# A graph and convolution layer on one core: residual add in each batch's turn, prefetch across groups, sums and norms in small pieces

## The chip, the cores and the metric

The kernel runs on one core of a Trainium2 chip. TensorE (PE) multiplies matrices, VectorE (DVE), ScalarE (ACT) and GpSimd (POOL) do the elementwise work, and SyncE (SP) issues all DMAs here from one queue. Each engine works through its own list of instructions in the order in which the program wrote them. The metric is device time in microseconds for one execution, the median of several runs.

## What is computed

Input `x` has 32 batches of 512 positions by 256 channels; `adj` is a 0/1 mask of 512 by 512 for each batch. All is in float32.

```python
h = maximum(layernorm(x), 0)                    # h is the layer's input; x the residual
# branch 1: convolution along the positions
c = relu(bn1(conv1d(h, conv1_w)))               # 1 tap
x_conv = relu(bn2(conv1d(c, conv2_w, pad=8)) + h)   # 17 taps, then the residual add
# branch 2: message passing
s = h @ w_se.T + b_se                           # 3 numbers for each position
A = exp(-|s_n - s_m|^2) * adj
x_nmp = A @ relu(h @ w_msg.T + b_msg)
# gated unit over both
gi = concat(x_conv, x_nmp) @ w_ih.T + b_ih;  gh = h @ w_hh.T + b_hh
r, z = sigmoid(...), sigmoid(...);  n = tanh(gi_n + r * gh_n)
out = x + (1 - z) * n + z * h
```

## The kernel before

The 32 batches are worked in 8 groups of 4 (`G`). Three kinds of work are written for each group:

- `rows(g)`: for each batch of group g, load `x` (`load`, L91), normalise it on DVE (`norm`, L174), transpose it on PE (`norm_t`, L189), store the transposed `h` to DRAM (`HD`), and run the 1-tap convolution (`conv1`, L201) into the tile `h1`, which holds one whole group.
- `convolution()` (L368): the 17-tap convolution of a whole group by a nested interpolation scheme with 5 x 5 products. DVE makes the operands `x2` from `h1`, four ahead; weights come from DRAM (`w<-wd`), two ahead; PE multiplies into `ps_c` (three buffers). `summed(g)` (L311) is a generator that takes each of the 25 products from PSUM and sums them into `y`. After the 25th, it evicts `y` to `xconv` for all four batches on ACT (L357, two instructions for each batch), then adds `h` on DVE (L361) and applies ReLU on ACT (L362). For this add, `h` of each batch is loaded from DRAM again (`load_h`, L99) into the tile `hTb`, which has two buffers.
- `rest(b, following)` (L478): all else for one batch. `positions` (L423) makes the tiles `left` and `right`, each partly on DVE (L426, L427) and partly as squares on ACT (L428, L429). Then come `messages` (L431), `kernel_exp` (L442, a matmul of `left` and `right` and an exponential on ACT), `finish` of the batch before (L460), `masked` (L447: transposes of the mask, multiplied in on DVE), the gather and the gates (L520 to L557), of which three elementwise operations for each half are on POOL (L552 to L554). After `masked`, the mask (`load_adj`, one buffer) and `h` of the `following` batch are loaded. The last batch of a group has no `following`.

The order is written out by hand: the main loop (L605 to L653) takes a step of `convolution()` for group g or of `others(g)` (the `rest` of group g-1 and `rows(g+1)`), in proportion to their estimated TensorE time. In `others(g)`, three batches' `rest` come first, then `rows(g+1)`, then the fourth `rest`. So the instructions of a group's last convolution step are followed by the four evictions, and then by `positions` of the group's first batch. Groups 1 to 6 repeat this in the same form. At the end, the four batches of the last group run through `rest` alone.

Of the kernel before, what the change touches and what calls it, by code (L numbers as in the profile page):

```python
# [8 lines left out]
F32 = mybir.dt.float32  # L9
# [31 lines left out]
def kernel(  # L41
# [47 lines left out]
    XS, MS, HB, XR = {}, {}, {}, {}  # L89

    def load(b):  # L91
        XS[b] = front.tile([P, NT, D], F32, name="x_sb")
        nc.sync.dma_start(XS[b], x[b].rearrange("(c p) d -> p c d", p=P))

    def load_adj(b):
# [4 lines left out]
        HB[b] = late.tile([P, ND, N], F32, name="hTb", bufs=2)  # L100
        nc.sync.dma_start(HB[b], HD[b])

    load(0)
    load(1)
    vec = const.tile([P, _NCOL], F32)
    nc.sync.dma_start(vec, vecs)
    w1 = const.tile([P, ND, D], F32)
# [63 lines left out]
    HT = {}  # L171
    HD = {b: dram.tile([P, ND, N], F32, name=f"hd{b}") for b in range(B)}

    def norm(b):  # L174
        xs = XS[b]
        st = front.tile([P, NT, 6], F32, name="st")
        mv = front.tile([P, NT, 2], F32, name="mv")
        for c in range(NT):
            nc.vector.bn_stats(st[:, c, :], xs[:, c, :])
            nc.vector.bn_aggr(mv[:, c, :], st[:, c, :])  # L180
        rstd = front.tile([P, NT], F32, name="rstd")
        rsqrt(rstd, mv[:, :, 1])
        for c in range(NT):
            nc.vector.tensor_scalar(  # L184
                xs[:, c, :], xs[:, c, :], mv[:, c, 0:1], rstd[:, c : c + 1],
                op0=ALU.subtract, op1=ALU.mult,
            )

    def norm_t(b, d):  # L189
        xn = XS[b]  # L190
        if d == 0:
            HT[b] = front.tile([P, ND, N], F32, name="hT")
        ps = tr.tile([P, N], F32, name="ps_tr")
        for c in range(NT):
# [110 lines left out]
    def weights_again():  # L305
        for n in range(25):
            w = cv.tile([P, 2, ND, D], F32, name="w", bufs=3)
            nc.sync.dma_start(w, WD[n])
            yield w

    def summed(g):  # L311

        y = cv.tile([P, 3, 3, NZ], F32, name="y")
        for j1 in ORDER:
            z = y[:, 0] if j1 == 3 else cv.tile([P, 3, NZ], F32, name="z")
            ends = z[:, 0:3:2, :]
# [3 lines left out]
            ps = yield  # L320
            nc.vector.tensor_tensor(z[:, 0, :], ps, n3, op=ALU.add)  # L321
            ps = yield
            nc.vector.scalar_tensor_tensor(z[:, 2, :], n3, 4.0, ps, op0=ALU.mult, op1=ALU.add)
            ps = yield
            n2 = cv.tile([P, NZ], F32, name="n", bufs=3)
            nc.scalar.activation(n2, ps, AF.Copy)
            ps = yield
            s = cv.tile([P, NZ], F32, name="s")
            nc.vector.tensor_tensor(s, ps, n2, op=ALU.add)
            nc.vector.tensor_tensor(n2, ps, n2, op=ALU.subtract)  # L330
            nc.vector.tensor_tensor(ends, ends, s[:, None, :].to_broadcast([P, 2, NZ]), op=ALU.add)  # L331
            nc.vector.scalar_tensor_tensor(z[:, 1, :], n3, 2.0, n2, op0=ALU.mult, op1=ALU.add)
            zf = z.rearrange("p e n -> p (e n)")
            yf = y.rearrange("p f e n -> p f (e n)")
            if j1 == 3:
                nc.scalar.activation(yf[:, 1], zf, AF.Copy, scale=2.0)
                nc.scalar.activation(yf[:, 2], zf, AF.Copy, scale=4.0)
            elif j1 == 0:
                nc.vector.tensor_tensor(yf[:, 0], yf[:, 0], zf, op=ALU.add)
            elif j1 == 4:  # L340
                nc.vector.tensor_tensor(yf[:, 2], yf[:, 2], zf, op=ALU.add)
            else:
                ye = yf[:, 0:3:2, :]
                nc.vector.tensor_tensor(
                    ye, ye, zf[:, None, :].to_broadcast([P, 2, 3 * NZ]), op=ALU.add
                )
                nc.vector.tensor_tensor(  # L347
                    yf[:, 1], yf[:, 1], zf, op=ALU.subtract if j1 == 2 else ALU.add
                )
        if late is None:  # L350
            late_pools()
        for b in range(g * G, (g + 1) * G):
            load_h(b)
            xc = XC[b] = late.tile([P, ND, 9 * U], F32, name="xconv", bufs=4)
            for o in range(ND):
                c = o * NU + b % G * U
                nc.scalar.activation(  # L357
                    xc[:, o, :].rearrange("p (u e f) -> p f e u", e=3, f=3), y[:, :, :, c : c + U],
                    AF.Identity, bias=bn2_sh[:, o : o + 1], scale=bn2_sc[:, o : o + 1],
                )  # L360
            nc.vector.tensor_tensor(xc[:, :, :N], xc[:, :, :N], HB.pop(b), op=ALU.add)  # L361
            nc.scalar.activation(xc[:, :, :N], xc[:, :, :N], AF.Relu)  # L362
        yield

    AHEAD, AHEAD_W = 4, 2
# [2 lines left out]
    def convolution():  # L368

        x2s, ws = [], []  # L370

        def all_operands():
            for _ in range(NG):
                yield from operands()

        def all_weights():
            yield from weights_first()
            for _ in range(NG - 1):
                yield from weights_again()

        xs, wg = all_operands(), all_weights()
        for g in range(NG):
            sums = summed(g)
            next(sums)
            done = None
            for n in range(25):
                while len(ws) < min(25 * g + n + 1 + AHEAD_W, 25 * NG):
                    ws.append(next(wg))

                while len(x2s) < min(25 * g + n + 1 + AHEAD, 25 * NG):  # L390
                    if len(x2s) == 25 * (g + 1):
                        yield "rows", g + 1
                    x2s.append(next(xs))
                    if len(x2s) == 25 * g + 21:
                        yield "free", g
                w, x2 = ws[25 * g + n], x2s[25 * g + n].rearrange("p (r v) -> p r v", v=V)
                ps = cps.tile([P, NZ], F32, name="ps_c")
                for o in range(ND):
                    matmul_sum(
                        ps[:, o * NU : (o + 1) * NU].rearrange("p (b u) -> p b u", u=U),  # L400
                        [
                            (w[:, k, i, o * P : (o + 1) * P], x2[:, i * G : (i + 1) * G, k : k + U])
                            for k in range(2)
                            for i in range(ND)
                        ],
                    )
                    if o == 0 and done is not None:
                        sums.send(done)
                    yield "pe", 1.65
                ws[25 * g + n] = x2s[25 * g + n] = None  # L410
                done = ps
            sums.send(done)
            yield "group", g
# [64 lines left out]
    def rest(b, following):  # L478
# [7 lines left out]
        xnmp = late.tile([P, ND, N], F32, name="xnmp")  # L486
        positions(b)
        yield 1.75
        for c in range(0, NT, 2):
            messages(b, msg, c)  # L490
            yield 1.8
# [12 lines left out]
        if following is not None:  # L504
            load_adj(following)
            load_h(following)
        hT, xconv = HB.pop(b), XC.pop(b)
        o_sb = late.tile([P, ND, N], F32, name="o_sb")
        x_in = [xconv[:, i, :N] for i in range(ND)] + [xnmp[:, i, :] for i in range(ND)]

        def cols(o, g):
            return slice(g * D + o * P, g * D + (o + 1) * P)
# [44 lines left out]
            yield 3.46  # L557
        waiting.append((b, o_sb))

    def rows(g):  # L560

        bs = list(range(g * G, (g + 1) * G))
        for b in bs[:2]:
            if b not in XS:
                load(b)
            norm(b)
        yield 0.0
        for n, b in enumerate(bs + [None]):
            if b is not None:
                for d in range(ND):  # L570
                    norm_t(b, d)
                    yield 0.55
            if n > 0:
                for o in range(ND):
                    conv1(bs[n - 1], o)
                    yield 1.73
            if n + 2 < G:
                load(bs[n + 2])
                norm(bs[n + 2])


    bn1_sc, bn1_sh = bn_affine("bn1")
# [3 lines left out]
        brz, vec[:, _COL["b_ih"] : _COL["b_ih"] + 2 * ND], vec[:, _COL["b_hh"] : _COL["b_hh"] + 2 * ND],  # L586
        op=ALU.add,
    )
    for _ in rows(0):
        pass  # L590

    def others(g):


        bs = list(range((g - 1) * G, g * G)) if g > 0 else []
        for b in bs[:-1]:
            yield from rest(b, b + 1)
# [112 lines left out]
```

## Time and profile before

| | |
|---|---|
| median of 3 runs | 2826.82 us (2824.49 to 2827.24) |
| the profiled execution's own time | 2832.12 us |
| its span, first to last instruction | 2830.3 us |
| PE busy | 2429.8 us, 86% |
| DVE, ACT, POOL busy | 1233.2, 651.2, 310.0 us |
| mean granted TensorE clock | 0.931 |

The profile describes one execution. Its own time is 5.3 us above the median of the runs, and 1.8 us of it lie outside the span. Busy shares are averages over eight groups, the start and the tail.

### The profile page before, as it was taken

To read this page: it belongs to the slowest core of one execution; us is meant where nothing else is said; L and a number is where in the kernel's file an instruction comes from. 1 tells how busy PE (TensorE), PEld (TensorE's weight loads), DVE (VectorE), ACT (ScalarE), POOL (GpSimd) and SP (SyncE) were. 2 spreads that over 40 slices of the span, in tenths; PEclk is the share of its full clock that TensorE was granted. 3 is DMA by queue.
4 is the path that set the end of the run, shared out by engine and by line. 5 is a ranking of instruction groups with operands and counts; after the bars stand their busy time and mean duration, and the time that the engine had idled before them with its cause. 6 is when DMAs were issued, how large, how long until landed. Compare 5 with 4: busy or idle time off the path is not lost.

```text
span 2830.3 us, 20941 instructions
## 1 busy us (share of the span) xinstructions
PE 2429.8 (86%) x8192; PEld 1498.6 (53%) x8192; DVE 1233.2 (44%) x1750; ACT 651.2 (23%) x882; POOL 310.0 (11%) x240
## 2 busy tenths in 40 slices
PE   6568998789986999959989599895998969995998
PEld 4555555456653665536656366563665546653444
DVE  7973345333453344534444434434344444433211
ACT  3232212122122211222212321123222132113221
POOL 1000111101111011011110111100111001111111
PEclk9888998889998999979999899998999989998999
DMA  4242223122232222222232222322223132212210
GB/s 184 104 160 91 88 74 104 60 97 82 89 104 83 80 82 97 90 82 82 82 104 82 90 86 95 101 75 97 82 82 104 60 104 89 82 52 67 75 37 23
DMA packets 113605, 247.95 MB, mean 88 GB/s; under 512 B 8930, under 2 KB 58210, under 8 KB 112866
## 3 DMA queue, kind: packets, MB, share of 16 engines
q1 hardware_dynamic: 113506, 246.60, 25.4%
q8 instruction: 65, 1.06, 0.2%
q14 instruction: 34, 0.28, 0.0%
HBM read 199.91 MB, written 46.66 MB: 87 GB/s over the span
## 4 chain that ended last, share of the span: by engine, by line
PE 77%; DVE 14%; ACT 4%; issue 3%; DMA 2%; POOL 1%; POOLq 0%; SPq 0%; DVEq 0%; ACTq 0%
PE ps_acc L86 49%; PE ps_c L86 18%; PE ps_tr L452 3%; PE ps_acc L444 3%; PE ps_tr L86 2%; DVE x L217 2%; ACT xconv L357 2%; PE ps_tr L195 2%; DVE x L220 1%; DMA hTb<-hd 1%; DVE xconv L361 1%; DVE y L347 1%; DVE z L331 1%; DVE y L468 1%; ACT xconv L362 1%
## 5 line engine op out<-in xcount | busy, mean ns | idle before, releaser
L86 PEld LDWEIGHTS ps_c<-x,w 128*128 128x128 f32 x3200 | 620.7, 195 | 182.1 <-issue 150.1
L86 PE MATMUL ps_c<-x,w 128*128 128x228 f32 x3200 | 694.4, 363 | 24.2 <-DVE z L321 8.2
L86 PE MATMUL ps_acc<-hTb,whh 128*128 128x512 f32 x768 | 361.8, 596 | 0.0
L86 PE MATMUL ps_acc<-xconv,wih 128*128 128x512 f32 x768 | 360.8, 592 | 0.0
L86 PE MATMUL ps_acc<-xnmp,wih 128*128 128x512 f32 x768 | 360.6, 592 | 0.0
L552 POOL TENSOR_TENSOR gate_t<-hTb,r 128x512 f32<-128x512 f32 x64 | 92.4, 1444 | 2276.4 <-ACT r L546 1510.2
L86 PE MATMUL ps_tr<-hTb,wse 128*67 128x512 f32 x128 | 74.3, 711 | 227.6 <-DMA hTb<-hd 200.2
L533 DVE SCALAR_TENSOR_TENSOR r<-ps_acc,vec,r 128x512 f32<-128x512 f32 x64 | 48.1, 751 | 449.9 <-ACT r L531 449.9
L86 PEld LDWEIGHTS ps_acc<-xnmp,wih 128*128 128x128 f32 x768 | 145.3, 189 | 184.3 <-issue 184.3
L86 PEld LDWEIGHTS ps_acc<-xconv,wih 128*128 128x128 f32 x768 | 145.8, 190 | 157.3 <-issue 156.9
L86 PE MATMUL ps_acc<-at,msg 128*128 128x512 f32 x512 | 228.5, 592 | 0.0
L545 DVE TENSOR_TENSOR r<-ps_acc,r 128x512 f32<-128x512 f32 x64 | 44.3, 692 | 399.9 <-PE ps_acc L86 399.7
L86 PEld LDWEIGHTS ps_acc<-hTb,whh 128*128 128x128 f32 x768 | 145.2, 192 | 115.3 <-issue 114.5
L531 ACT ACT_TABLE_LOAD x32 | 41.1, 1283 | 642.0 <-PE ps_acc L86 642.0
L220 DVE SCALAR_TENSOR_TENSOR x<-x,x 128x471 f32<-128x471 f32 (+1 forms) x184 | 158.5, 861 | 5.3
L86 PEld LDWEIGHTS ps_tr<-hTb,wse 128*67 128x67 f32 x128 | 19.5, 160 | 263.1 <-DMA hTb<-hd 205.9
L217 DVE TENSOR_TENSOR x<-x 128x471 f32<-128x471 f32 x200 | 157.7, 807 | 1.4
L86 PEld LDWEIGHTS ps_acc<-at,msg 128*128 128x128 f32 x512 | 97.2, 190 | 106.4 <-issue 106.2
L458 DVE COPY xnmp<-ps_acc 128x512 f32<-128x512 f32 x64 | 44.3, 692 | 246.6 <-PE ps_acc L86 246.6
L444 PE MATMUL ps_acc<-right,left 67*128 67x512 f32 x256 | 124.5, 614 | 14.7 <-ACT at L445 8.7
L195 PE MATMUL ps_tr<-ident,x_sb 128*128 128x128 f32 x256 | 56.3, 365 | 89.8 <-DVE x_sb L184 68.5
L541 ACT ACTIVATE z<-ps_acc,brz 128x512 f32<-128x512 f32 x64 | 44.0, 687 | 337.1 <-PE ps_acc L86 337.1
(94 smaller groups left out, 2312.0 us busy)
## 6 DMA issues: line engine op xcount, KB each, us to landing
w<-wd SPq DMA_DIRECT2D x175, 512.0 KB, 3.3
hTb<-hd SPq DMA_DIRECT2D x64, 512.0 KB, 5.1
m_sb<-in_adj_dram SPq DMA_DIRECT2D x32, 1024.0 KB, 5.6
x_sb<-in_x_dram SPq DMA_DIRECT2D x32, 512.0 KB, 4.4
hd<-hT SPq DMA_DIRECT2D x32, 512.0 KB, 2.9
y<-in_x_dram SPq DMA_DIRECT2D x64, 256.0 KB, 4.0
out_dram<-y SPq DMA_DIRECT2D x64, 256.0 KB, 2.3
wd<-w SPq DMA_DIRECT2D x25, 512.0 KB, 2.8
```

The costliest lines, as they stand in the source:

```text
L86: nc.tensor.matmul(ps, lhsT, rhs, start=(i == 0), stop=(i == len(pairs) - 1))
L195: nc.tensor.transpose(ps[:, c * P : (c + 1) * P], xn[:, c, d * P : (d + 1) * P], ident)
L217: nc.vector.tensor_tensor(dst, get(a), get(b), op=ALU.subtract)
L220: nc.vector.scalar_tensor_tensor(dst, a, -2.0, b, op0=ALU.mult, op1=ALU.add)
L357: nc.scalar.activation(xc[:, o, :].rearrange("p (u e f) -> p f e u", e=3, f=3), y[:, :, :, c : c + U], AF.Identity, bias=bn2_sh[:, o : o + ...
L444: nc.tensor.matmul(ps, left[:, c * P : (c + 1) * P], right, start=True, stop=True)
L452: nc.tensor.transpose(ps[:, n * P : (n + 1) * P], m[:, n, c * P : (c + 1) * P], ident)
L458: nc.vector.tensor_copy(xnmp[:, d, :], ps)
L533: nc.vector.scalar_tensor_tensor(r, ps_h, vec[:, _COL["b_hh"] + 2 * ND + o : _COL["b_hh"] + 2 * ND + o + 1], r, op0=ALU.add, op1=ALU.mult,)
L541: nc.scalar.activation(z, ps_z, AF.Sigmoid, bias=brz[:, ND + o : ND + o + 1])
L545: nc.vector.tensor_tensor(r, ps_n, r, op=ALU.add)
L552: nc.gpsimd.tensor_tensor(t, hT[:, o, :], r, op=ALU.subtract)
```

## The change

It does the following:

- `x_sb` gets three buffers in place of two, and three batches are loaded at the start.
- `norm` becomes a generator that yields between pieces of two to four DVE instructions. `rows_begin(g)` loads the first three batches of a group and enters their norms in `NORMS`; it is called when `rest` of the third batch begins. Each step of `others` first issues one piece (`norm_some`). `norm_all` issues what is left when the batch is transposed. The fourth batch is loaded and entered inside `rows`.
- In `summed`, the additions that do not read PSUM are entered in `SUMS`. One piece is issued at each second half of a convolution step, the remainder before the next products that need the tile `z`, and all of them at the end of the group. Where one addition wrote two thirds of `y` and a second the last third, there are now three.
- The residual add and its ReLU move from `summed` into `rest`, behind `positions`, with the `h` that `rest` has anyway. The separate loads of `h` in `summed` go.
- The last batch of a group now has the next group's first batch as `following`, so its mask and `h` are loaded after `masked` of the last batch.

```diff
     def load(b):
-        XS[b] = front.tile([P, NT, D], F32, name="x_sb")
+        XS[b] = front.tile([P, NT, D], F32, name="x_sb", bufs=3)
...
-    load(0)
-    load(1)
+    for b in range(3):
+        load(b)
...
+    NORMS = {}
+
     def norm(b):
...
             nc.vector.bn_aggr(mv[:, c, :], st[:, c, :])
+            if c % 2:
+                yield
         rstd = front.tile([P, NT], F32, name="rstd")
         rsqrt(rstd, mv[:, :, 1])
+        yield
         for c in range(NT):
...
+            if c % 2:
+                yield
+
+    def norm_some(pieces=1):
+
+        for b in list(NORMS):
+            while pieces and b in NORMS:
+                pieces -= 1
+                if next(NORMS[b], "done") == "done":
+                    del NORMS[b]
+
+    def norm_all(b):
+        if b in NORMS:
+            for _ in NORMS.pop(b):
+                pass
 
     def norm_t(b, d):
         xn = XS[b]
         if d == 0:
+            norm_all(b)
...
+    SUMS = []
+
+    def sum_some(pieces=1):
+        while SUMS and pieces:
+            SUMS.pop(0)()
+            pieces -= 1
+
     def summed(g):
...
             ps = yield
+            sum_some(len(SUMS))
+            z = y[:, 0] if j1 == 3 else cv.tile([P, 3, NZ], F32, name="z")
...
-            nc.vector.tensor_tensor(ends, ends, s[:, None, :].to_broadcast([P, 2, NZ]), op=ALU.add)
-            nc.vector.scalar_tensor_tensor(z[:, 1, :], n3, 2.0, n2, op0=ALU.mult, op1=ALU.add)
+            add(ends, ends, s[:, None, :].to_broadcast([P, 2, NZ]))
+            twice(z[:, 1, :], n3, n2)
...
-                ye = yf[:, 0:3:2, :]
-                nc.vector.tensor_tensor(
-                    ye, ye, zf[:, None, :].to_broadcast([P, 2, 3 * NZ]), op=ALU.add
-                )
-                nc.vector.tensor_tensor(
-                    yf[:, 1], yf[:, 1], zf, op=ALU.subtract if j1 == 2 else ALU.add
-                )
+                for e in range(3):
+                    add(yf[:, e], yf[:, e], zf, ALU.subtract if (e, j1) == (1, 2) else ALU.add)
+        sum_some(len(SUMS))
...
         for b in range(g * G, (g + 1) * G):
-            load_h(b)
...
-            nc.vector.tensor_tensor(xc[:, :, :N], xc[:, :, :N], HB.pop(b), op=ALU.add)
-            nc.scalar.activation(xc[:, :, :N], xc[:, :, :N], AF.Relu)
...
                     if o == 0 and done is not None:
                         sums.send(done)
+                    else:
+                        sum_some()
                     yield "pe", 1.65
...
         positions(b)
         yield 1.75
+        xc = XC.pop(b)
+        xconv = xc[:, :, :N]
+        nc.vector.tensor_tensor(xconv, xconv, HB[b], op=ALU.add)
+        nc.scalar.activation(xconv, xconv, AF.Relu)
         for c in range(0, NT, 2):
             messages(b, msg, c)
...
+    def rows_begin(g):
+
+        for b in range(g * G, g * G + 3):
             if b not in XS:
                 load(b)
-            norm(b)
-        yield 0.0
+            NORMS[b] = norm(b)
+
+    def rows(g):
+
+        bs = list(range(g * G, (g + 1) * G))
...
+                if n == 0:
+                    load(bs[3])
+                    NORMS[bs[3]] = norm(bs[3])
...
-            if n + 2 < G:
-                load(bs[n + 2])
-                norm(bs[n + 2])
...
+    rows_begin(0)
     for _ in rows(0):
-        pass
+        norm_some()
...
-        for b in bs[:-1]:
+        for n, b in enumerate(bs[:-1]):
+            if n == 2 and g + 1 < NG:
+                rows_begin(g + 1)
             yield from rest(b, b + 1)
+        if not bs:
+            rows_begin(g + 1)
         yield "rows wanted", g + 1
...
         for b in bs[-1:]:
-            yield from rest(b, None)
+            yield from rest(b, b + 1)
...
+            norm_some()
             got = next(other, None)
```

## Rows read from the trace of the kernel before

**Rows 1.** The page, part 1: busy us (share of the span) and instructions.
```profile
PE 2429.8 (86%) x8192; PEld 1498.6 (53%) x8192; DVE 1233.2 (44%) x1750; ACT 651.2 (23%) x882; POOL 310.0 (11%) x240
```
**Rows 2.** Waits over the whole span: who waited for whom, us, times, longest.
```profile
PE ps_tr L86 <- DMA hTb<-hd: 200.2, 7, 29.7
...
PE ps_tr L195 <- DVE x_sb L184: 68.5, 9, 14.6
...
PE ps_tr L86 <- issue: 27.4, 1, 27.4
...
PE ps_tr L195 <- issue: 21.3, 9, 2.7
```
**Rows 3.** Timeline over one group's end: start us, us, instruction, [idle before, releaser].
```profile
537.98 29.81 SPq L101 DMA_DIRECT2D hTb<-hd  x4
...
548.91 0.62 DVE L329 TENSOR_TENSOR s<-ps_c,n 128x456 f32<-128x456 f32 x1
...
549.89 1.27 POOL L552 TENSOR_TENSOR gate_t<-hTb,r 128x512 f32<-128x512 f32 x1 [17.27 <-ACT r L546]
...
553.76 3.95 DVE L344 TENSOR_TENSOR y<-y,z 128x2736 f32<-128x2736 f32 x1
557.64 1.57 DVE L347 TENSOR_TENSOR y<-y,z 128x1368 f32<-128x1368 f32 x1
559.24 2.35 ACT L357 ACTIVATE xconv<-y,bn_shift,bn_scale 128x513 f32<-128x513 f32 x2 [9.50 <-DVE y L347]
...
572.06 0.32 SPq L101 DMA_DIRECT2D hTb<-hd  x1
...
577.66 3.68 PE L86 MATMUL ps_tr<-hTb,wse 128*67 128x512 f32 x4 [29.40 <-DMA hTb<-hd]
...
582.87 0.68 ACT L428 ACTIVATE right<-ps_tr,bse 3x512 f32<-3x512 f32 x1 [5.15 <-DVE right L427]
...
588.59 3.60 PE L444 MATMUL ps_acc<-right,left 67*128 67x512 f32 x8
```
**Rows 4.** Timeline at the start of a group's rows.
```profile
784.53 1.70 PE L86 MATMUL ps_c<-x,w 128*128 128x228 f32 x8
...
792.27 2.30 PE L195 MATMUL ps_tr<-ident,x_sb 128*128 128x128 f32 x8 [6.03 <-DVE x_sb L184]
...
799.21 2.81 PE L86 MATMUL ps_c<-x,w 128*128 128x228 f32 x8
...
801.86 3.60 PE L86 MATMUL ps_acc<-hT,w 128*128 128x512 f32 x8
```
**Rows 5.** Timeline where the third batch's `rest` begins.
```profile
707.67 0.94 SPq L474 DMA_DIRECT2D y<-in_x_dram  x2
...
718.77 1.88 PE L86 MATMUL ps_tr<-hTb,wse 128*67 128x512 f32 x4
...
725.48 3.60 PE L444 MATMUL ps_acc<-right,left 67*128 67x512 f32 x8
...
731.84 1.25 PE L452 MATMUL ps_tr<-ident,m_sb 128*128 128x128 f32 x8 [0.35 <-DVE y L468]
```
**Rows 6.** Instructions grouped by line and shape: busy us, mean ns, idle before.
```profile
L179 DVE BATCH_NORM_STATS2 st<-x_sb 128x6 f32<-128x256 f32 x128 | 51.4, 401 | 22.2 <-DMA x_sb<-in_x_dram 22.0
...
L184 DVE TENSOR_SCALAR x_sb<-x_sb,mv,rstd 128x256 f32<-128x256 f32 x128 | 44.2, 410 | 37.2 <-POOL rstd L143 36.0 <-PE ps_acc L86 1.2
...
L361 DVE TENSOR_TENSOR xconv<-xconv,hTb 128x1024 f32<-128x1024 f32 x32 | 39.3, 1227 | 100.1 <-ACT xconv L357 100.1
...
L362 ACT ACTIVATE xconv<-xconv 128x1024 f32<-128x1024 f32 x32 | 33.9, 1058 | 41.4 <-DVE xconv L361 41.4
...
L180 DVE BATCH_NORM_AGGREGATE mv<-st 128x2 f32<-128x6 f32 x128 | 23.3, 182 | 4.4
```
**Rows 7.** Timeline at the start and inside the first group.
```profile
25.45 0.43 DVE L179 BATCH_NORM_STATS2 st<-x_sb 128x6 f32<-128x256 f32 x1 [5.12 <-DMA x_sb<-in_x_dram]
...
140.45 2.30 PE L195 MATMUL ps_tr<-ident,x_sb 128*128 128x128 f32 x8 [14.13 <-DVE x_sb L184]
```

More of the change, by code (lines that the diff above doesn't have):

```diff
@@ L309, in weights_again, with add, copy, twice @@
             yield w
+    SUMS = []
[3 more added lines that the diff above has]
+            pieces -= 1
     def summed(g):
         y = cv.tile([P, 3, 3, NZ], F32, name="y")
+        yf = y.rearrange("p f e n -> p f (e n)")
+        def add(dst, a, b, op=ALU.add):
+            SUMS.append(lambda: nc.vector.tensor_tensor(dst, a, b, op=op))
+        def copy(dst, src, scale):
+            SUMS.append(lambda: nc.scalar.activation(dst, src, AF.Copy, scale=scale))
+        def twice(dst, a, b):
+            SUMS.append(
+                lambda: nc.vector.scalar_tensor_tensor(dst, a, 2.0, b, op0=ALU.mult, op1=ALU.add)
+            )
         for j1 in ORDER:
-            z = y[:, 0] if j1 == 3 else cv.tile([P, 3, NZ], F32, name="z")
-            ends = z[:, 0:3:2, :]
             ps = yield
@@ L320, in summed @@
             ps = yield
+            sum_some(len(SUMS))
+            z = y[:, 0] if j1 == 3 else cv.tile([P, 3, NZ], F32, name="z")
+            ends = z[:, 0:3:2, :]
+            zf = z.rearrange("p e n -> p (e n)")
             nc.vector.tensor_tensor(z[:, 0, :], ps, n3, op=ALU.add)
@@ L330, in summed @@
             nc.vector.tensor_tensor(n2, ps, n2, op=ALU.subtract)
-            nc.vector.tensor_tensor(ends, ends, s[:, None, :].to_broadcast([P, 2, NZ]), op=ALU.add)
-            nc.vector.scalar_tensor_tensor(z[:, 1, :], n3, 2.0, n2, op0=ALU.mult, op1=ALU.add)
-            zf = z.rearrange("p e n -> p (e n)")
-            yf = y.rearrange("p f e n -> p f (e n)")
+            add(ends, ends, s[:, None, :].to_broadcast([P, 2, NZ]))
+            twice(z[:, 1, :], n3, n2)
             if j1 == 3:
[L336 to L341, printed above, removed]
-            else:
-                ye = yf[:, 0:3:2, :]
-                nc.vector.tensor_tensor(
-                    ye, ye, zf[:, None, :].to_broadcast([P, 2, 3 * NZ]), op=ALU.add
-                )
-                nc.vector.tensor_tensor(
-                    yf[:, 1], yf[:, 1], zf, op=ALU.subtract if j1 == 2 else ALU.add
-                )
+                copy(yf[:, 1], zf, 2.0)
+                copy(yf[:, 2], zf, 4.0)
+            elif j1 in (0, 4):
+                add(yf[:, j1 // 2], yf[:, j1 // 2], zf)
+            else:
+                for e in range(3):
+                    add(yf[:, e], yf[:, e], zf, ALU.subtract if (e, j1) == (1, 2) else ALU.add)
+        sum_some(len(SUMS))
         if late is None:
@@ L506, in rest @@
             load_h(following)
-        hT, xconv = HB.pop(b), XC.pop(b)
+        hT = HB.pop(b)
         o_sb = late.tile([P, ND, N], F32, name="o_sb")
-        x_in = [xconv[:, i, :N] for i in range(ND)] + [xnmp[:, i, :] for i in range(ND)]
+        x_in = [xconv[:, i, :] for i in range(ND)] + [xnmp[:, i, :] for i in range(ND)]
         def cols(o, g):
@@ L558, in rest @@
         waiting.append((b, o_sb))
+    def rows_begin(g):
+        for b in range(g * G, g * G + 3):
+            if b not in XS:
+                load(b)
+            NORMS[b] = norm(b)
     def rows(g):
         bs = list(range(g * G, (g + 1) * G))
-        for b in bs[:2]:
-            if b not in XS:
-                load(b)
-            norm(b)
-        yield 0.0
         for n, b in enumerate(bs + [None]):
```

## The prediction

> **What bounds the kernel now.** I read the page first: PE is busy 86% of the span and no other engine half of it [rows 1]. So time is won only where PE stands. The table of waits says where: the `positions` matmul that opens each group's first `rest` waits 200.2 us in seven cases, and 27.4 us in an eighth that the profile puts down to issue; the transposes of `rows` wait 68.5 us for the normalised `x`, and 21.3 us more in gaps put down to issue, nine of each [rows 2]. These four rows are 317 us. The reader is to see that the other waits of PE are small beside them, and that these come at two fixed places of each group, so I read a timeline at each.
>
> At a group's end [rows 3], PE runs out of work at 577.66 - 29.40 = 548.26. DVE then sums the last products (from 548.91), ACT starts the evictions at 559.24, and each batch waits in turn for its add and ReLU. SP stands for 29.81 us at the four loads of `h` for these adds, since `hTb` has two buffers. Behind them in SP's queue is the load of `h` that `positions` needs: it is issued at 572.06, and PE resumes at 577.66. So the wait is a chain DVE, ACT, DVE, SP and a DMA.
>
> At the start of the rows [rows 4], PE ends its convolution step at 784.53 + 1.70 = 786.2, and the first `conv1` runs at 801.86. The 15.6 us between hold two pairs of transposes and one convolution step, and two waits for a norm that DVE has only just begun.
>
> **The change part by part.**
>
> *Early load of the next first batch, residual add moved.* The loads of `h` for the adds, and with them SP's block, are gone, and the next batch's `h` is asked for after `masked` of the fourth batch, ahead of that batch's gather and gates. `positions` can run at 548.26. What is late next? `kernel_exp` needs the squares, which ACT has in its list behind all eight evictions. The sums of DVE are as long as before (three single additions at 1.57 us in place of 3.95 + 1.57), so the evictions start at 559.24. They no longer wait for adds: four pairs at 2.35 us end at 568.6, two squares at 0.68 us end at 570.0 [rows 3]. PE's own work until then: from `positions` to `kernel_exp` it needs 725.48 - 718.77 = 6.7 us with one convolution half-step between [rows 5]; here there are two, so 8.2 us, and it stands from 556.5 to 570.0, 13.5 us. `kernel_exp` ran at 588.59 [rows 3] and comes 18.6 us earlier.
>
> Of the clock: after the wait four matmuls of `positions` took 3.68 us [rows 3], against 1.88 us elsewhere [rows 5], so about half speed. I expect the same after 13.5 us: `kernel_exp` then takes about 7.0 us in place of 3.6, which gives back 3.4. Left: 15.2 us for each of six groups. The first group's end is alike, with more loads beside it: 15. The last has no convolution left, so PE has 5.2 us of work before `kernel_exp` and stands 16.5 of the 21.7 us; against the mean wait of 200.2 / 7 = 28.6, with 1.6 us of slower clock on balance, 10.5.
>
> *Norms ahead of the rows.* Three norms are spread over the third batch's `rest`: each has six pieces (one of them empty), 18 in all, and about 22 steps follow `rows_begin` there, so they are issued in time. Their loads stand in SP's queue right behind the loads of `y` at 707.67, 11 us before `positions` of that batch [rows 5]; what SP has behind them are weights for later steps. With the norms done, PE from 786.2 needs two pairs of transposes at about 1.15 (half of the 2.30 at low speed), some 0.5 for an eviction and 1.70 for the convolution step [rows 4]: 4.5 in place of 15.6. Gain 11.1 in each of six groups. The fourth batch's load and norm lie beside the transposes and `conv1` of the batches before it; I give them nothing. Without that cover they would cost what the load waited in the start (5.12 us, [rows 7]) and the 3.7 us of a norm (below).
>
> What do the norms cost where they go? One batch is (51.4 + 23.3 + 44.2) / 32 = 3.7 us of DVE [rows 6]. Most steps of `rest` are long matmuls beside which DVE is idle. But in `finish` and `masked`, PE waits for DVE's read of each tile already (0.35 us in [rows 5]), and some five pieces fall there, 2 x 1.17 for statistics and 2 x 0.82 for the scaling, with a small one between: 4.3 us. Bounds: 0, if DVE catches up, and 11.1, all three batches. I take 4.3.
>
> *The moved add in the bodies.* In each `rest` DVE gets 1.23 us and ACT 1.06 us [rows 6] ahead of the messages' evictions. Behind them wait `kernel_exp`'s buffers and exponentials. Bounds 0 and 2.3 for each batch; I take 2.0 a group for the three batches not at a boundary, since DVE is less than half busy. In [rows 3] an addition of 2736 elements beside the POOL gate operations took 3.95 us, and one of half the size, after them, 1.57: 0.8 us more than twice. The moved add comes right after the previous batch's last gates, so this may be added to it; the 2.0 has room for one or two such cases. The Trainium skill (SBUF — State Buffer, "Who interferes with whom") speaks against the place: a VectorE instruction with two SBUF inputs contends with a GpSimd instruction that reads SBUF, and the loser is blocked for all of the other's instruction. By the row it is 0.8 us for a batch; by the rule it could be a whole gate operation, 1.27 us in [rows 3], so some 2 us more in a group, 12 in all.
>
> *Sums in pieces.* The DVE work is the same within a microsecond. That a clump no longer stands ahead of `finish` may help, that pieces fall elsewhere may hurt; I take nothing; the clump's own 3.95 + 1.57 us [rows 3] bounds it for a group, either way.
>
> *Start and first group.* The third batch's load, on which DVE waits 5.12 us [rows 7], is issued first; some 1 us of it goes to the small loads that now stand behind it, so I take 4. In the first group the transposes waited 14.13 us [rows 7] for a load and a norm that both begin at that point; now the load is early but the first norm still is not: 5.5, between 0 and 9. The last group and the tail have only the moved adds: 3 lost.
>
> **Sum.** 6 x (15.2 + 11.1 - 4.3 - 2.0) = 120; with 15 + 10.5 + 5.5 + 4 - 3 it is 152. The profiled execution took 2832.1, so 2680; it stood 5.3 above the median, so **2675 us**.
>
> **The rivals.**
>
> *A, the forecast:* 2675, own range 2640 to 2705.
>
> *B, PE runs through the group's end.* If the squares get to ACT before the evictions, the remaining 13.5 us and the slow 3.4 go too: 7 x 16.9 + 20 = 138 more, 2537. Against it: both stand in ACT's list in that order, and in [rows 3] the squares (582.87) come last. Chance 0.07.
>
> *C, DVE becomes the bound in the third batch.* All three norms exposed: 6 x (11.1 - 4.3) = 41 more, 2716. For it: `masked` is paced by DVE already; against: DVE's 44%. 0.17.
>
> *D, slower: the norms wait for their loads.* The pieces stand in DVE's list, so if SP holds the loads of `x` behind a weight load that waits for its buffer, DVE stands, and PE after it. SP was held 29.81 us once a group [rows 3]. From 152 / 6 = 25 us a group the gain is gone; at 30 the time would be 2675 + 180 = 2855. Against it: SP got to the place 11 us ahead of PE [rows 5]. 0.03.
>
> *E, the boundary does not move.* If `h` of the next batch landed no earlier, because SP's queue holds it, only the rows gain: 2675 + 6 x 15.2 + 25.5 = 2792. Its queue is free once the four loads go, so 0.04.
>
> **How the numbers follow.** A has 0.68; B 0.07, C 0.17, E 0.04, D 0.03, and 0.01 that all cancels. The range takes in C and, below, what the costs could fall to: 38 if norms and adds were hidden (6 x 6.3), 27 if the clock did not fall (8 x 3.4), not both at once. Low 2630, high 2722. About 0.2% is what a measurement can tell here; faster by more has A, B, C and E: 0.96; within 0.2%: 0.01; slower: 0.03.
>
> **What would show it.** In the table of waits, `positions` should wait for no DMA any more, and `kernel_exp` for ACT's squares, some 13 us in each of seven cases and 16 in the last. The evictions should stand back to back for 9.4 us. At the rows, PE should not wait for `x_sb` in groups 1 to 6. At the third batch, PE's waits in `masked` should grow by some 4 us. If `kernel_exp` waits under 5 us, B holds; if PE waits over 10 us more in the third batch, C; if DVE's statistics wait for DMA there, D. Each of groups 1 to 6 should be some 20 us shorter.

## The result and the profile after

The changed kernel takes 2666.38 us (median of 4 runs, 2665.11 to 2667.98) beside 2825.65 us for the kernel before on the same chip: a ratio of 0.9441, 95% interval 0.9424 to 0.9458. The forecast was 2675. The profiled execution has a span of 2665.4 us and a mean granted clock of 0.949; `kernel_exp` is L480 now, the transposes of `rows` L217, those of `masked` L488, the moved add L527.

The page's part 1, as [rows 1]:

```profile
PE 2441.9 (92%) x8192; PEld 1505.2 (56%) x8192; DVE 1228.8 (46%) x1766; ACT 640.5 (24%) x882; POOL 328.6 (12%) x240
```

PE's waits, as [rows 2]: who waited for whom, us, times, longest.

```profile
PE ps_acc L480 <- ACT left L465: 99.2, 9, 16.0
PE ps_tr L217 <- DVE x_sb L190: 25.4, 2, 16.6
PE ps_tr L488 <- DVE y L504: 17.9, 19, 1.8
PE ps_acc L480 <- ACT at L481: 15.8, 15, 1.4
...
PE ps_tr L86 <- DMA hTb<-hd: 9.9, 1, 9.9
...
PE ps_tr L217 <- issue: 5.2, 2, 2.7
```

The four rows of 317 us have become 9.9, 25.4 and 5.2 (issue). What the reader is to see is the new first row: `kernel_exp` waits for ACT's `left`, 99.2 us. The kernel before has this row too, but it is short there:

```profile
PE ps_acc L444 <- ACT left L429: 5.0, 2, 3.3
```

So 94 us of it are new: 13.0 us at six groups' ends and 16.0 at the last. The first group's end has none of it; there `positions` waits the 9.9 us for `h`, which SP asks for only behind the gates' weights.

The timeline of the group's end that answers to [rows 3]:

```profile
508.14 1.88 PE L86 MATMUL ps_tr<-hTb,wse 128*67 128x512 f32 x4
...
508.95 0.62 DVE L374 TENSOR_TENSOR s<-ps_c,n 128x456 f32<-128x456 f32 x1
...
513.82 5.52 DVE L347 TENSOR_TENSOR y<-y,z 128x1368 f32<-128x1368 f32 x3
...
519.37 8.76 ACT L393 ACTIVATE xconv<-y,bn_shift,bn_scale 128x513 f32<-128x513 f32 x8 [9.58 <-DVE y L347]
...
528.15 0.68 ACT L464 ACTIVATE right<-ps_tr,bse 3x512 f32<-3x512 f32 x1
528.84 0.68 ACT L465 ACTIVATE left<-ps_tr,bse 3x512 f32<-3x512 f32 x1
529.55 1.06 ACT L528 ACTIVATE xconv<-xconv 128x1024 f32<-128x1024 f32 x1
...
529.58 7.20 PE L480 MATMUL ps_acc<-right,left 67*128 67x512 f32 x8 [13.02 <-ACT left L465]
...
536.56 2.69 PE L86 MATMUL ps_c<-x,w 128*128 128x228 f32 x8
```

`positions` runs with no wait and at 1.88 us. ACT's eight evictions then stand back to back, and the two squares come behind them; only then can `kernel_exp` go. It runs at the lower of the clock's two levels (1.2 of 2.4 GHz: granted 0.50 from 529.6 to 536.6 us), and so does most of the convolution step behind it (granted 0.61; 2.69 us in place of the 1.70 in [rows 4]).

PE's timeline where the third batch's `rest` begins, as [rows 5], and at the start of the rows, as [rows 4]:

```profile
665.47 1.88 PE L86 MATMUL ps_tr<-hTb,wse 128*67 128x512 f32 x4
...
675.85 1.12 PE L480 MATMUL ps_acc<-right,left 67*128 67x512 f32 x2 [0.93 <-ACT at L481]
...
681.18 0.66 PE L488 MATMUL ps_tr<-ident,m_sb 128*128 128x128 f32 x4 [1.79 <-DVE y L504]
682.88 1.97 PE L488 MATMUL ps_tr<-ident,m_sb 128*128 128x128 f32 x8 [1.04 <-DVE y L504]
685.41 1.11 PE L488 MATMUL ps_tr<-ident,m_sb 128*128 128x128 f32 x4 [0.56 <-DVE at L489]
...
739.15 1.03 PE L217 MATMUL ps_tr<-ident,x_sb 128*128 128x128 f32 x8
740.44 1.15 PE L217 MATMUL ps_tr<-ident,x_sb 128*128 128x128 f32 x8 [0.25 <-ACT hT L218]
741.42 1.71 PE L86 MATMUL ps_c<-x,w 128*128 128x228 f32 x8
742.96 3.60 PE L86 MATMUL ps_acc<-hT,w 128*128 128x512 f32 x8
```

In the third batch these waits of PE are 0.93 + 1.79 + 1.04 + 0.56 = 4.3 us; the kernel before has 0.6 us at the same place (0.35 of it in [rows 5]). The first transposes and `conv1` follow each other with no wait for `x_sb`.

To compare kernels by stage, I took the start of each batch's four-matmul `positions` row from the timelines, 24 intervals over six groups (from the first batch of the second group worked in `others` to that of the last group), and averaged each stretch. The group's end stands before `positions` in the kernel before and behind it in the others, so the fourth and first batch's stretches are added. The third stretch holds the rows, in five groups of the six. The period is the sum, the time of one group. Each row is one execution, the profiled one; that of the kernel before stood 6 us above its median, the others within 2.3 us of theirs, so a difference against the first row can be up to 1 us a period too large. In us:

| kernel | 4th + 1st | 2nd | 3rd | period |
|---|---|---|---|---|
| before | 171.3 | 70.3 | 97.3 | 338.8 |
| after | 155.1 | 71.9 | 92.8 | 319.8 |
| e1_add: the add and the early load alone | 159.1 | 72.7 | 97.5 | 329.3 |
| e2_norm: the norms alone | 171.4 | 70.2 | 90.6 | 332.1 |
| e3_sums: the sums in pieces alone | 166.9 | 70.2 | 99.4 | 336.5 |
| e7_quiet | 155.3 | 74.3 | 87.8 | 317.4 |
| e8_fill | 152.9 | 71.8 | 92.3 | 317.1 |
| e10_add_later | 154.9 | 70.0 | 91.4 | 316.3 |
| e5_late_evict | 146.9 | 70.1 | 90.5 | 307.5 |
| e6_late_sums | 141.5 | 70.2 | 92.2 | 303.9 |
| e9_both | 141.1 | 70.2 | 87.5 | 298.7 |
| e12_finish_later | 139.8 | 70.7 | 86.9 | 297.5 |

### The profile page after: what moved, and what is told of

Its sections match the earlier page's. It is cut to its first block, busy times and chain, and to the rows that moved or that the text cites. A ratio compares the mean times of both kernels' runs of the same rounds, so it can differ in the third digit from the quotient of the medians.

```text
span 2665.4 us, 20881 instructions
## 1 busy us (share of the span) xinstructions
PE 2441.9 (92%) x8192; PEld 1505.2 (56%) x8192; DVE 1228.8 (46%) x1766; ACT 640.5 (24%) x882; POOL 328.6 (12%) x240
## 4 chain that ended last, share of the span: by engine, by line
PE 80%; DVE 12%; ACT 4%; issue 2%; DMA 1%; POOL 1%; SPq 0%; POOLq 0%; DVEq 0%; ACTq 0%
PE ps_acc L86 51%; PE ps_c L86 20%; PE ps_acc L480 4%; ACT xconv L393 2%; PE ps_tr L488 2%; DVE x L239 2%; PE ps_tr L86 2%; DVE y L347 1%; PE ps_tr L217 1%; DVE x L242 1%; PE ps_tr L500 1%; DVE at L489 1%; DVE st L182 1%; DVE y L504 1%; DVE z L347 1%
## 5 line engine op out<-in xcount | busy, mean ns | idle before, releaser
L480 PE MATMUL ps_acc<-right,left 67*128 67x512 f32 x256 | 155.3, 739 | 120.8 <-ACT left L465 99.2
L480 PEld LDWEIGHTS ps_acc<-right,left 67*128 67x128 f32 x256 | 54.5, 225 | 185.6 <-ACT left L465 102.5
L586 ACT ACTIVATE r<-r,vec 128x512 f32<-128x512 f32 x64 | 46.2, 722 | 307.5 <-DVE r L585 307.5
L86 PE MATMUL ps_acc<-hT,w 128*128 128x512 f32 x256 | 119.1, 607 | 0.0
```

The source lines that it names most:

```text
L86: nc.tensor.matmul(ps, lhsT, rhs, start=(i == 0), stop=(i == len(pairs) - 1))
L480: nc.tensor.matmul(ps, left[:, c * P : (c + 1) * P], right, start=True, stop=True)
L586: nc.scalar.activation(r, r, AF.Tanh, bias=vec[:, _COL["b_ih"] + 2 * ND + o : _COL["b_ih"] + 2 * ND + o + 1],)
```

## The experiments: each part alone

Times are medians; the kernel before took 2824.5 to 2829.0 us beside them.

**e1_add.** The kernel before, with the residual add moved and the early load:

```diff
         for b in range(g * G, (g + 1) * G):
-            load_h(b)
...
-            nc.vector.tensor_tensor(xc[:, :, :N], xc[:, :, :N], HB.pop(b), op=ALU.add)
-            nc.scalar.activation(xc[:, :, :N], xc[:, :, :N], AF.Relu)
...
         positions(b)
         yield 1.75
+        xc = XC.pop(b)
+        xconv = xc[:, :, :N]
+        nc.vector.tensor_tensor(xconv, xconv, HB[b], op=ALU.add)
+        nc.scalar.activation(xconv, xconv, AF.Relu)
...
-            yield from rest(b, None)
+            yield from rest(b, b + 1)
```

> The kernel before with the moved residual add and the early load of the next group's first batch alone. Theory (the forecast's terms): 6 x 15.2 + 15 + 10.5 at the groups' ends, less 6 x 2.0 + 3 for the adds in the bodies, so 102 off 2826: about 2724; PE's wait for squares some 13 us at each group's end, the waits of the rows as before (68 us). Rival 1, one wait only takes the place of another (the parts are worth much less or more alone than together): under 60 or over 140 off.

Measured: 2750.05 us, ratio 0.9739 (0.9722 to 0.9756), so 74 us won where 102 were expected. By the table the end of a group gains 12.1 us (171.27 - 159.13) in place of 15.2, and the second batch loses 2.4.

**e2_norm.** The kernel before, with three `x_sb`, `norm` in pieces, `rows_begin` and `norm_some` as in the change and nothing else:

```diff
-        for b in bs[:-1]:
+        for n, b in enumerate(bs[:-1]):
+            if n == 2 and g + 1 < NG:
+                rows_begin(g + 1)
...
+            norm_some()
             got = next(other, None)
```

> The kernel before with the norms spread ahead and three buffers for x alone. Theory: 6 x (11.1 - 4.3) + 5.5 + 4, so 50 off: about 2776; no wait for x_sb in groups 1 to 6, some 4 us more of waits in masked of each third batch; the wait of positions as before (200 us). Rival 1: under 25 or over 80 off.

Measured: 2768.51 us, 0.98 (0.9785 to 0.9815): 56 us won. The third stretch is 97.3 - 90.6 = 6.7 us shorter on the mean, 8.0 in each of the five groups that have rows.

**e3_sums.** The kernel before, with the sums that do not read PSUM issued in pieces:

```diff
+            add(ends, ends, s[:, None, :].to_broadcast([P, 2, NZ]))
+            twice(z[:, 1, :], n3, n2)
...
                     if o == 0 and done is not None:
                         sums.send(done)
+                    else:
+                        sum_some()
```

> The kernel before with the sums in pieces alone. Theory: nothing, 2826 within 6 us. Rival 2, the clump of sums held PE's small waits in masked and kernel_exp: 10 to 25 us off (up to 3 us in each of 8 groups).

Measured: 2807.22 us, 0.9935 (0.9917 to 0.9954): 17 us won; the rival held. The reason stands in the kernel before, and most plainly in its last group, where this wait is longest. DVE's and PE's rows of its timeline there:

```profile
2520.60 3.01 DVE L344 TENSOR_TENSOR y<-y,z 128x2736 f32<-128x2736 f32 x1
2523.53 1.58 DVE L347 TENSOR_TENSOR y<-y,z 128x1368 f32<-128x1368 f32 x1
2525.02 0.68 DVE L468 TENSOR_TENSOR y<-ps_tr,y 128x512 f32<-128x512 f32 x1
...
2525.76 3.08 PE L452 MATMUL ps_tr<-ident,m_sb 128*128 128x128 f32 x12 [6.99 <-DVE y L468]
```

DVE's list has the clump ahead of the small addition of `finish` (L468), and the mask's transposes wait 6.99 us for the buffer that this addition reads. The same wait, in the table of waits of the kernel before and then of e3_sums:

```profile
PE ps_tr L452 <- DVE y L468: 28.2, 29, 7.0
```

```profile
PE ps_tr L469 <- DVE y L485: 8.5, 23, 0.9
```

It falls by 19.7 us. That this is near the 17 us gained is a coincidence. The gain is larger where the wait was: 3.3 us in the fourth batch of each of five groups and 9 us in the last, since matmuls behind a wait also run at the lower clock. And 2.5 us a group are lost again at the rows, where an addition of the sums now stands in DVE's list ahead of the first norm, so that the wait of 6.03 us [rows 4] grows. Both in e3_sums:

```profile
772.65 2.64 DVE L325 TENSOR_TENSOR y<-y,z 128x1368 f32<-128x1368 f32 x1
```

```profile
779.96 2.30 PE L195 MATMUL ps_tr<-ident,x_sb 128*128 128x128 f32 x8 [7.83 <-DVE x_sb L184]
```

**e4_no_ahead.** The changed kernel without the early load of the mask and `h` for a group's first batch:

```diff
-            yield from rest(b, b + 1)
+            yield from rest(b, None)
```

> The changed kernel without the early load for the last batch of a group: mask and h of the next first batch are asked for when its turn begins. Theory: SP's queue is free there, the loads land some 4 us after PE wants them, and PE waits for the squares until 13 us later anyway, so nothing is lost: 2664 to 2674, positions late by some 4 us and kernel_exp at the same place. Rival 3, the early load is what removes the wait: positions 8 us or more late with all behind it, 7 x 8 = 56 more, about 2722.

Measured: 2665.76 us, 0.9439 (0.9424 to 0.9453), the changed kernel's time. With the add's loads gone from SP's queue, the ordinary load comes in time: `positions` waits for a DMA at the first group's end alone (9.8 us), as in the changed kernel. The early load is worth nothing that can be measured.

The parts alone give 74 + 56 + 17 = 147 us, the whole change 159. In the six periods of the table they add up to within 0.6 us each; where the rest of the 12 us comes from, no run shows.

## The experiments: what holds the changed kernel

**e5_late_evict.** The evictions are issued behind the exponentials' matmul of the next group's first batch (and before the sums first write a new `y`), the add and ReLU behind the mask's products:

```diff
+            if j1 == 3:
+                evict_all()
+                y = cv.tile([P, 3, 3, NZ], F32, name="y")
...
-        for b in range(g * G, (g + 1) * G):
+        def evict():
+            for b in range(g * G, (g + 1) * G):
...
+        EVICT.append(evict)
...
         positions(b)
         yield 1.75
-        xc = XC.pop(b)
...
+            if c == NT - 1:
+                evict_all()
...
+        xc = XC.pop(b)
```

> The changed kernel with the eight evictions of a group issued behind kernel_exp of its first batch (the residual add behind masked), so that the squares stand ahead of them in ACT's list. Theory (ACT's order holds kernel_exp for the 9.4 us of evictions, DVE's sums for the rest): the wait for squares falls from 13 to about 5 us, 8 x 8 less a little given back in masked: about 2606. Rival 4, DVE's sums or the slow clock hold it: the wait stays above 10 us, 2650 or more.

Measured: 2581.48 us, 0.9138 (0.9122 to 0.9154), 85 us less than the changed kernel. Some 27 of them are the place of the add (e10_add_later below), so the evictions' place is worth some 58. `kernel_exp` at a group's end in e5_late_evict, PE's timeline:

```profile
516.49 7.19 PE L491 MATMUL ps_acc<-right,left 67*128 67x512 f32 x8 [5.61 <-ACT left L476]
```

13.02 has become 5.61, and `kernel_exp` still runs at the lower clock (granted 0.50): the squares now wait only for DVE's `left` and `right`, which stand behind the last sums.

**e6_late_sums.** e5_late_evict, and the group's last sums are issued behind the first batch's messages:

```diff
-        sum_some(len(SUMS))
...
+            if c == NT - 2 and EVICT:
+                sum_some(len(SUMS))
```

> As the run before, and the last sums of a group are not flushed at its end but behind the first batch's messages. Theory: left and right and the squares come first on DVE and ACT, so kernel_exp no longer waits and the clock does not fall there; the sums then delay finish and masked by 3 to 5 us a group: 8 x (13 + 3.4 - 4), about 2567. Rival 4: the time lost moves whole into finish and masked, where PE waits for the same sums: no better than the run before.

Measured: 2551.81 us, 0.9032 (0.9017 to 0.9046). `kernel_exp` and the mask's transposes at the same place in e6_late_sums:

```profile
514.91 3.60 PE L490 MATMUL ps_acc<-right,left 67*128 67x512 f32 x8
...
524.62 3.94 PE L498 MATMUL ps_tr<-ident,m_sb 128*128 128x128 f32 x16 [3.69 <-DVE y L514]
```

`kernel_exp` has no wait and runs at 3.60 us (granted clock 1.00). The sums delay `finish` instead, 3.69 us, and the transposes behind that wait run at a granted clock of 0.50. The two runs together win 115 us on the changed kernel. Some 27 of them are the place of the add; the other 88 are the group's end, by the table 155.1 - 141.5 = 13.6 us in each of six groups: 13.0 of wait and 4.6 of slow matmuls, less the 3.7 that `finish` now waits and a little for the slow transposes behind it.

**e7_quiet.** The changed kernel, with the norms begun one batch earlier and no piece issued from `kernel_exp` to `masked`:

```diff
+        quiet = True
...
+        quiet = False
...
-            if n == 2 and g + 1 < NG:
+            if n == 1 and g + 1 < NG:
...
-            norm_some()
+            if not quiet:
+                norm_some()
```

> The changed kernel with no norm pieces in the steps of kernel_exp, finish and masked (they begin one batch earlier, so that as many steps remain). Theory: the 4.3 us of waits in masked of each third batch go: 6 x 4.3, about 2640. Rival 5, the norms cost where they stand, whatever the step: no gain, 2660 to 2672, the waits turning up at other steps.

Measured: 2652.1 us, 0.9388 (0.937 to 0.9407), between the two. The third batch gains 5.0 us (6.1 in each of the five groups with rows), the second loses 2.4: there the norms stand beside the messages, whose evictions `kernel_exp` needs. Its row of waits in e7_quiet, 5.8 us in the changed kernel:

```profile
PE ps_acc L480 <- DVE msg L475: 14.9, 6, 3.8
```

**e8_fill.** The changed kernel, with 14 matmuls whose result nobody reads ahead of the first batch's `kernel_exp`:

```diff
+        if b % G == 0:
+            junk = tr.tile([P, N], F32, name="ps_tr")
+            for i in range(FILL):
+                nc.tensor.matmul(junk, wmsg[:, 0, :P], HB[b][:, 0, :], start=True, stop=True)
```

> The changed kernel with 14 matmuls without use (about 12 us at full speed) ahead of kernel_exp of each group's first batch, in the time in which PE waits for the squares. They add work and leave nothing out. Theory: the clock does not fall, kernel_exp takes 3.6 in place of 7.2 us after the wait: 8 x 3.4 = 27 less, about 2639; or, where ACT's exponentials then hold the fourth kernel_exp, half of that, 2652. Rival 6, the low clock there costs nothing since ACT is behind anyway, or the filling runs over the wait: 2666 or more.

Measured: 2658.79 us, 0.9412 (0.9397 to 0.9427): 7.6 us won, less than either of the theory's two figures. PE's timeline at the group's end in e8_fill (the 28 and 8 matmuls of the profile are 14 and 4 in the kernel):

```profile
525.08 12.18 PE L536 MATMUL ps_tr<-hTb,wmsg 128*128 128x512 f32 x28
538.37 2.84 PE L481 MATMUL ps_acc<-right,left 67*128 67x512 f32 x6 [1.11 <-ACT left L466]
542.40 1.24 PE L481 MATMUL ps_acc<-right,left 67*128 67x512 f32 x2 [1.19 <-ACT at L482]
543.43 3.25 PE L87 MATMUL ps_c<-x,w 128*128 128x228 f32 x8
```

Six of the eight matmuls of `kernel_exp` take 2.84 us in place of some 5.4 (three quarters of 7.20), but the last two wait for the exponentials, which free their buffers, and the convolution step behind is slow all the same (3.25). It ends 542.40 + 1.24 - 516.83 = 26.8 us after its `positions` began (that row starts at 516.83); in the changed kernel it is 529.58 + 7.20 - 508.14 = 28.6. With part of the clock back, ACT is the limit; the fall came later, and was not avoided.

The 7.6 us are also less than what the filling wins where there is a gap. At the first group's end `kernel_exp` does not wait, so the filling is pure cost there: its first batch takes 81.9 us in place of 70.3. The same place in the changed kernel and then in e8_fill:

```profile
206.00 3.60 PE L480 MATMUL ps_acc<-right,left 67*128 67x512 f32 x8
```

```profile
204.30 12.18 PE L536 MATMUL ps_tr<-hTb,wmsg 128*128 128x512 f32 x28
216.31 3.60 PE L481 MATMUL ps_acc<-right,left 67*128 67x512 f32 x8
```

Without these 11.6 us it would be some 2647 us, an estimate, between the theory's two figures.

**e10_add_later.** The changed kernel, with only the add and ReLU moved behind the mask's products:

```diff
         positions(b)
         yield 1.75
-        xc = XC.pop(b)
-        xconv = xc[:, :, :N]
-        nc.vector.tensor_tensor(xconv, xconv, HB[b], op=ALU.add)
-        nc.scalar.activation(xconv, xconv, AF.Relu)
...
+        xc = XC.pop(b)
+        xconv = xc[:, :, :N]
+        nc.vector.tensor_tensor(xconv, xconv, HB[b], op=ALU.add)
+        nc.scalar.activation(xconv, xconv, AF.Relu)
```

> The changed kernel (2666.4 us) with one edit: the moved residual add and its ReLU stand behind the mask's products of the same batch, no longer right behind the positions; the evictions at a group's end stay where they are. Theory: the add beside the previous batch's gate operations costs about 2.5 us in the second batch of each of six groups, and its ReLU of 1.06 us stands in ScalarE's list ahead of the work that the exponentials' matmul of a group's first batch needs. Both go: 6 x 3.5 = 21, so about 2645 us, between 2640 and 2650, and the second batch takes 69.6 us again in place of 72.1. Rival: the cost only shifts to the place to which the add moves, and the time stays at 2660 or more.

Measured: 2639.17 us, 0.9329 (0.9316 to 0.9343): 27 us less. The second batch takes 70.0 us again, the third gains 1.4. One half of the theory fell: the first batch does not gain (87.7 us against 87.8 from its `positions` to the next), since the ReLU already stood behind the squares at 529.55. The second batch's gate operation and add in the changed kernel, from its timeline:

```profile
597.64 2.64 POOL L594 TENSOR_TENSOR o_sb<-r,gate_t 128x512 f32<-128x512 f32 x1
...
597.95 1.20 DVE L527 TENSOR_TENSOR xconv<-xconv,hTb 128x1024 f32<-128x1024 f32 x1
...
599.68 2.58 DVE L239 TENSOR_TENSOR x<-h 128x1415 f32<-128x1415 f32 x1
```

and the same gate operation and `x<-h` in e10_add_later, where the add is not beside them:

```profile
593.43 1.27 POOL L594 TENSOR_TENSOR o_sb<-r,gate_t 128x512 f32<-128x512 f32 x1
...
594.74 2.11 DVE L239 TENSOR_TENSOR x<-h 128x1415 f32<-128x1415 f32 x1
```

**e9_both.** e6_late_sums, with norm pieces only beside the gather and the gates, from the second batch on (`quiet` from `positions` to the end of `masked`; otherwise the diff of e7_quiet).

> The kernel with late evictions and late last sums (2551.8 us) with one more edit: pieces of the norms are issued only beside a batch's gather and gates, from the second batch on, and none between positions and the end of the mask's products. Theory: the 4 to 5 us that PE waits in each third batch for VectorE's reads of mask tiles go, 6 x 4.5 = 27, so 2522 to 2530 us. Rival: as when the same was done to the changed kernel alone, only some 14 us are won, since the norms delay something in the second batch instead: 2538 us or more.

Measured: 2520.95 us, 0.8915 (0.89 to 0.8929): 31 us less than e6_late_sums, a little more than the theory's 27. The third batch falls from 92.2 to 87.5 us and the second stays at 70.2.

**e12_finish_later.** e9_both, with `finish` of the previous batch behind the gather:

```diff
-        while waiting:
-            for c in range(0, NT, 2):
-                finish(*waiting[0], c)
-                yield 0.55
-            waiting.pop(0)
...
+                while waiting:
+                    for c in range(0, NT, 2):
+                        finish(*waiting[0], c)
+                        yield 0.55
+                    waiting.pop(0)
```

> The kernel before this one in the same call (late evictions, late last sums, norms beside gather and gates) with one more edit: the second matrix product's remainder for the previous batch (finish) stands behind the gather and no longer just ahead of the mask's transposes. Theory: there PE waits for VectorE's read of each tile, 3.7 us a group behind the last sums and some more elsewhere, 42 us in all; moved to a stretch in which VectorE is idle, most of it goes: about 25 us less than the kernel without this edit, some 2500 us. Rival: the wait moves to the transposes of the mask that follow, which VectorE paces too, and the time is the same within 5 us.

Measured: 2506.72 us, 0.886 (0.8847 to 0.8873): 14 us less, between the theory and the rival. The waits of the mask's transposes, in e9_both and then in e12_finish_later:

```profile
PE ps_tr L498 <- DVE y L514: 30.9, 23, 4.1
...
PE ps_tr L498 <- DVE at L499: 10.0, 21, 3.7
```

```profile
PE ps_tr L498 <- DVE at L499: 34.0, 20, 4.1
```

Of 40.9 us, 34.0 stay: most of the wait only changed its releaser. About half of the gain shows in the six periods (1.2 us each); the rest lies ahead of them and in the tail. This is the fastest of the kernels here: 322 us less than the kernel before (2828.98 beside it) and 160 less than the changed one. PE is busy 2382.6 of its 2502.6 us span, 95%.

## Why the prediction came out right, point by point

The time was 9 us below the forecast, but that it came so near is in part luck: the terms erred both ways. By part, forecast and measured alone: add and early load 6 x (15.2 - 2.0) + 15 + 10.5 - 3 = 102, measured 74; norms 6 x (11.1 - 4.3) + 5.5 + 4 = 50, measured 56; sums 0, measured 17. That is 152 against 147, and the parts win 12 more together.

- **The chain at the group's end: the mechanism was right.** `positions` has no wait, `kernel_exp` waits for the squares behind the eight evictions, 13.02 us (13.5 forecast), and takes 7.20 (7.0). This holds at six groups' ends and, with 16.0 us (16.5 forecast), at the last.
- **Its gain, 15.2, was sized too large: 12.1.** `kernel_exp` was costed from the one group end that I read, with a wait of 29.4; the mean over seven is 28.6 [rows 2], 0.8 less. The clock's price was ended at `kernel_exp`, but the next convolution step is slow too, 2.69 in place of 1.70: 1.0. Some 1.3 us of the rest I have not placed.
- **The moved add, 2.0 a group, was too small: 3.5.** e10_add_later takes 1.9 us out of the second batch and 1.4 out of the third, so about 6 x 3.5 = 21 of its 27. Of the mechanism the prediction had the place right (beside the previous batch's gates) and the row wrong: not the VectorE addition grew, as in [rows 3], but the GpSimd operation, from 1.27 to 2.64; the add itself took 1.20. The longer gate operation then lay beside the next VectorE operation, 2.58 in place of 2.11, and the second eviction of the messages came 1.2 us later behind `positions` than in e10_add_later: 0.7 for the add's own place in DVE's list, 0.5 for that slower operation. The Trainium skill (SBUF — State Buffer, "Who interferes with whom") has the loser blocked for all of the other's instruction. The 1.37 us by which the GpSimd operation grew agree with that: the add took 1.20. By the same section of the Trainium skill the first to issue wins; in the trace the GpSimd operation starts first (597.64, the add 597.95) and loses, so there the trace differs. The prediction's figure by that rule, 2 us more in a group, is nearer than the one by the row, but partly by luck, since the add's own time is in the measured cost.
- **The norms.** 4.3 us in the third batch were forecast, and the trace has 4.3, but that the two agree is luck: 0.6 us of these waits stand in the kernel before as well, the 0.93 for ACT is gone once the add is moved (e10_add_later), and the matmuls behind the waits also run slower, for which the term had nothing. By e7_quiet the norms' place costs 6.1 us in each of the table's five groups with rows. At the rows the wait is gone, as forecast. Rival C (all three exposed) fell, and so did D: PE waits for no load there. e7_quiet shows that these microseconds are not bound to the work: away from the mask's transposes the norms cost the third batch 5.0 less, but 2.4 more in the second while the add stood there. In e9_both, where the add is elsewhere and no piece stands beside the messages either, only the gain is left; which of the two brings that, no run shows.
- **Sums in pieces, taken as 0: 17.** This is the step that failed. The sentence that the clump stands ahead of `finish` named the place; but the row for it, 28.2 us of waits for `finish`, was counted among the small waits and left out of the sum. The bound by the clump's 5.5 us held in most groups (a wait of 2.0) and not in the last, where the wait alone was 6.99. e3_sums settles it: the row falls to 8.5.
- **Early load: no value of its own** (e4_no_ahead). The prediction gave the gain to two edits together; it belongs to the add's loads that left SP's queue.
- **The rest.** First group: a wait of 8.8 us is left of the 14.13 [rows 7], so 5.3 won (5.5 forecast). Convolution begins 3.2 us earlier (4). At the first group's end `positions` still waits 9.9 us for `h`, where it waited 27.4 [rows 2]: 17.5 won (15). That the size fits is luck: the prediction had this end alike with the others, with no wait for a DMA and 13 us for the squares, and neither came. The two batches on either side of the last group's end take 159.6 us before and 141.6 after, 18.0 less (10.5), with the clump's 6.99 us in it. What comes behind them is 0.4 longer (3). The six periods of the table are 19.0 us shorter (some 20).
- **Rivals B and E** are answered by the same row: `kernel_exp` does wait 13 us (against B), and the boundary did move (against E). e5_late_evict and e6_late_sums then bring B about by their order of issue; its further gain, put at 138, is some 88 there.

## What to carry to other kernels

Where a stage is freed, look at what the next instruction needs and where that stands in its engine's list: here a wait for a DMA became one behind eight evictions, and putting two short squares ahead of them was worth some 58 us, another 2% (e5_late_evict against e10_add_later). Cost a small wait at a place that recurs in each batch as its row in the table of waits says, not as nothing, when the edit removes what releases it. A move that gains at one place and loses at another (the norms, beside the messages) should be tried again when its neighbour has moved, before it is called worth little.

## What was not expected of the hardware

- A VectorE add of two SBUF operands beside a GpSimd operation on SBUF took no longer (1.20 us; 1.23 on average in [rows 6]), while the GpSimd operation took 2.64 in place of 1.27 us. In [rows 3] a VectorE addition beside the GpSimd operation below was the longer one (3.95 us; 3.01 at 2520.60, where none is beside it). In both cases the GpSimd operation had started first, so either side can lose, and the order of the starts in the trace does not tell which.

```profile
553.32 1.53 POOL L554 TENSOR_TENSOR o_sb<-r,gate_t 128x512 f32<-128x512 f32 x1
```

- The granted clock fell to its lower level after waits much shorter than the 13 us: in e5_late_evict `kernel_exp` still took 7.19 us, at a granted clock of 0.50, after a wait of 5.61. In e6_late_sums, with no wait ahead of it, it took 3.60, but the transposes after the wait of 3.69 ran at 0.50. A gap's price is its length and the slow matmuls behind it, and here it was halved without those getting any faster.
- Filling the gap with matmuls (e8_fill) kept the clock up for `kernel_exp` alone (granted 1.00): the step behind it took 3.25 us at 0.50. The filling won 2.2 us at each of six groups' ends and lost 11.6 at the first, where there was no gap.
